# Two cross attentions on one core: two pairs of PSUM banks in turn for scores, values and transposes, later values, and the other work four products ahead

## The chip, the core and the metric

The kernel runs on one core of a Trainium2 chip. The metric is device time in microseconds from the first to the last instruction of one launch, with what the runtime adds around it; lower is better. A core has five engines, each with its own queue that it works through in order: TensorE (in profiles PE, with its weight loads as PEld), VectorE (DVE), ScalarE (ACT), GpSimd (POOL) and SyncE (SP). DMAs are issued from the queues of SP, POOL and ACT. Matmuls write PSUM, 8 banks of 128 partitions x 512 numbers; everything else lies in SBUF or in device memory.

## What is computed

Two cross attentions, one after the other, on x of 4 batches x 1024 rows x 1024 columns (4096 rows in all) against a context of 4 x 64 rows, all in float32:

```
# layer 0: 32 query heads of 32 columns in 8 groups that share keys and values
q, k, v = x @ Wq + bq, ctx @ Wk + bk, ctx @ Wv + bv
p   = softmax(q k^T / sqrt(32) + mask)            # 64 keys
x1  = layernorm((p v) @ Wo + bo + x) * gamma + beta
# layer 1: 16 heads of 64 columns, keys and values from layernorm(ctx)
Q, K, V = x1 @ Wq'^T, a @ Wk'^T, a @ Wv'^T        # a = layernorm(ctx)
p   = softmax(Q K^T / 8, masked)
y   = x1 + tanh(gate) * ((p V) @ Wo'^T)
```

## The kernel before

**Tiling.** The rows are worked on in subtiles of 128 (`SUB` = 8 of them make one of four blocks, `NSUB` = 32 in all). Large products use a scheme with seven block products in place of eight: sums of blocks are made on VectorE, and TensorE multiplies 128 x 512 blocks. A set-up stage makes keys and values and the queries of block 0. Then comes the loop of the first attention, in `mix` (L721). After it the output projection of layer 0 runs over 16 pairs of subtiles (L961), and then scores, softmax and output of layer 1, pair by pair (L1077).

**The loop of the first attention.** `mix(t, steps)` writes down the attention of subtile t and strews other TensorE work between its parts: in blocks 0 to 2 the 28 steps of the next block's query products (`query_steps`, L535; each step is four matmuls of 128 x 512, L541), dealt out 3 or 4 to a subtile, and in block 3 the five steps of `folded_queries` (L822) that turn a chunk of the second layer's query weight on TensorE and multiply it with the keys. `other()` (L728) runs a share of the steps.

Subtile t itself: `front(c)` (L637), for c = 0 and 1, computes half of the scores into a `big` tile (eight matmuls of 64 x 128, L644) and VectorE adds the mask and moves them to SBUF (L648). `largest` finds maxima (L655) and subtracts part of them (L658); `powers` runs the exponentials on ScalarE (L662, L670); `total` sums (L675) and `divide` multiplies with the reciprocal (L679). Then the probabilities have to be turned so that keys lie on partitions. Up to subtile 20 (`by_turning`, L603) they go to device memory (L773, on POOL's queue) and come back as `pq` in quarters (L694, POOL again), and `flip` turns 32 x 32 squares on VectorE (L381). From subtile 21 on `flip` uses transposes on TensorE (L704) and copies on ScalarE (L705). `values(c)` multiplies with the values (L710), copies (L716) and stores the result (L717, SP).

In `mix(t)`, `outputs0(t - 1)` is called after the first score half, so the loads of `pq` stand there; `flip(0)` and `flip(1)` of subtile t-1 stand in the middle, `values(0)` and `values(1)` of t-1 behind the sums and divisions of t.

**PSUM.** Four banks (`wx`) serve the large products. Two single banks (`one`) serve values, transposes and half of the folded values (L860). One pair (`big`) serves both score halves and the other half of the folded values.

**Queries.** The queries of a block are stored to `qTd` by SP and loaded again subtile by subtile (L612), one subtile ahead. The first load of a block stands at the end of the last subtile of the block before (L771); in the first subtile of a block a sixth share of the steps stands ahead of the scores.

**What sets the order.** The order in the text is only a priority. A scheduler orders the instructions of each engine from these priorities, the buffers that are free, and durations of its own; so an engine's order can differ from the text by a subtile or more. It also puts in the waits.

## Time and profile before

| | us |
|---|---|
| runs (3) | 1973.22 median, 1964.64 to 1975.02 |
| the profiled run | 1974.35, of which 1972.6 is the span of its instructions |
| TensorE (PE) busy | 1914.1, 97% |
| VectorE (DVE) busy | 1276.1, 65% |
| ScalarE (ACT) busy | 395.8, 20% |
| GpSimd (POOL) busy | 295.1, 15% |
| mean granted TensorE clock | 0.986 of full |

The loop of the first attention lies from about 195 us (its first scores are at 196.8) to about 755 us (its last values end at 753.4); what follows it takes the rest of the span.

How to read the profile: a row of a timeline gives start and duration in us, the engine, the line of the kernel, the operation, output and input by the names of the tiles, and in brackets how long the engine had been idle before, and who released it. A float32 matmul appears as two rows, so eight score matmuls are sixteen rows. A row of the waits gives waiter and releaser, the sum in us, how often, and the longest. The chain of waits follows the work that ended last back through its releasers. The granted clock is the share of full speed that TensorE was given.

### The profile page before, as it was taken

Reading aid. Unit: us, or ns where it says so; the run is one execution under the profiler, and the core shown is the slowest. Engines: PE = TensorE matmul, PEld = TensorE weight load, DVE = VectorE, ACT = ScalarE, POOL = GpSimd, SP = SyncE. Lnnn points to the kernel's source line nnn. Section 1 sums busy time; section 2 is a strip of 40 time slices with the busy share of each in tenths; the row PEclk is TensorE's granted clock in tenths of the full one; section 3 lists DMA queues with packets and bytes.
Section 4 is the critical chain, followed back from the end, with each engine's and each line's share of the span. In section 5 each row is a group of like instructions: output and inputs, shape, how many; then the busy total and the mean of one; then the engine's idle time right before and its main releaser. Section 6 shows DMA issues by size and latency. Waiting matters only on the chain.

```text
span 1972.6 us, 16687 instructions
## 1 busy us (share of the span) xinstructions
PE 1914.1 (97%) x5872; PEld 888.8 (45%) x5872; DVE 1276.1 (65%) x1540; ACT 395.8 (20%) x1131; POOL 295.1 (15%) x208
## 2 busy tenths in 40 slices
PE   8999999998989899999999999999999999999998
PEld 7744443443434564443443444444444444444443
DVE  3524886887877885445467667657675766576653
ACT  1111652553534673212200000000000000000000
POOL 0000111121110102545555543000000000000000
PEclk9999999998999799999999999999999999999999
DMA  8971699686895688376483335456746574747421
GB/s 279 183 183 63 198 247 239 202 239 210 229 259 186 217 266 291 128 245 213 160 234 139 117 106 128 139 142 157 181 118 161 138 181 117 178 120 181 117 85 43
DMA packets 218917, 346.28 MB, mean 176 GB/s; under 512 B 25425, under 2 KB 140497, under 8 KB 213585
## 3 DMA queue, kind: packets, MB, share of 16 engines
q1 hardware_dynamic: 189824, 271.80, 48.6%
q0 software_dynamic: 9744, 44.05, 8.0%
q10 hardware_dynamic: 19264, 29.37, 5.4%
q8 instruction: 46, 0.75, 0.2%
q14 instruction: 39, 0.31, 0.1%
HBM read 205.44 MB, written 139.72 MB: 175 GB/s over the span
## 4 chain that ended last, share of the span: by engine, by line
PE 67%; DVE 6%; DMA 3%; issue 1%; ACT 1%; POOL 0%; SPq 0%; DVEq 0%; ACTq 0%; POOLq 0%
PE wx L405 58%; PE wx L541 3%; PE one L710 2%; PE one L863 1%; DVE sm L675 1%; PE big L644 1%; DVE s L679 1%; DVE mx L655 1%; PE one L704 1%; DVE s L648 1%; PE big L863 1%; PE wx L836 1%; DMA pq<-p 1%; DMA q<-qTd 1%; DMA xq<-in_x_dram 1%
## 5 line engine op out<-in xcount | busy, mean ns | idle before, releaser
L413 DVE TENSOR_TENSOR r<-wx,r 128x512 f32<-128x512 f32 x224 | 153.6, 686 | 262.0 <-PE wx L405 259.7
L467 ACT ACTIVATE s<-s 128x1024 f32<-128x1024 f32 x32 | 33.7, 1057 | 651.1 <-DVE s L466 642.7
L417 DVE TENSOR_TENSOR s<-wx,key_bias 128x512 f32<-128x512 f32 x64 | 44.1, 690 | 137.3 <-PE wx L405 137.3
L662 ACT ACTIVATE s<-s,mx 128x64 f32<-128x64 f32 x336 | 111.8, 334 | 60.4 <-DVE mx L655 55.8
L541 PE MATMUL wx<-xT,wq_S 128*128 128x512 f32 x256 | 121.7, 608 | 0.8 <-ACT z L552 0.8
L405 PE MATMUL wx<-wo_B,S 128*128 128x512 f32 x256 | 117.0, 599 | 0.4 <-DVE r L413 0.4
L888 POOL TENSOR_TENSOR r<-r,bo 128x1024 f32<-128x1024 f32 x32 | 78.8, 2470 | 256.0 <-DMA r<-in_x_dram 256.0
L541 PE MATMUL wx<-xB,wq_A 128*128 128x512 f32 x256 | 116.9, 599 | 0.0
L405 PE MATMUL wx<-b_B,pT 128*128 128x512 f32 x256 | 116.1, 593 | 0.1
L405 PE MATMUL wx<-b_B,S_p 128*128 128x512 f32 x256 | 115.9, 595 | 0.0
L405 PE MATMUL wx<-a_B,xT 128*128 128x512 f32 x256 | 115.4, 592 | 0.0
L405 PE MATMUL wx<-a_B,S_x 128*128 128x512 f32 x256 | 115.3, 593 | 0.0
L405 PE MATMUL wx<-wo_B,o 128*128 128x512 f32 x256 | 114.1, 596 | 0.0
L648 DVE TENSOR_TENSOR s<-big,m 128x1024 f32<-128x1024 f32 x64 | 77.5, 1211 | 56.3 <-PE big L644 53.5
L644 PE MATMUL big<-kv,q 64*128 64x128 f32 x1024 | 79.0, 291 | 19.9 <-DVE s L648 12.3
L929 POOL TENSOR_TENSOR r<-r,gamma 128x1024 f32<-128x1024 f32 x32 | 76.0, 2376 | 137.2 <-DVE r L285 137.2
L644 PEld LDWEIGHTS big<-kv,q 64*128 64x128 f32 x1024 | 67.2, 194 | 64.1 <-DVE s L648 30.9
L381 DVE STREAM_TRANSPOSE pT<-pq 128x1024 f32<-128x1024 f32 x70 | 82.7, 1217 | 0.0
L710 PE MATMUL one<-pT,kv 128*64 128x512 f32 x256 | 73.0, 667 | 9.0 <-DVE pT L381 8.9
L930 POOL TENSOR_TENSOR r<-r,beta 128x1024 f32<-128x1024 f32 x32 | 80.8, 2523 | 2.4
L679 DVE TENSOR_TENSOR s<-s,sm 128x1024 f32<-128x1024 f32 x64 | 78.7, 1248 | 0.5
L405 PEld LDWEIGHTS wx<-wo_B,S 128*128 128x128 f32 x256 | 47.2, 190 | 66.4 <-issue 54.4
(163 smaller groups left out, 3000.0 us busy)
## 6 DMA issues: line engine op xcount, KB each, us to landing
p<-s POOLq DMA_DIRECT2D x21, 1024.0 KB, 5.9
pq<-p POOLq DMA_DIRECT2D x84, 256.0 KB, 7.1
xq<-in_x_dram SPq DMA_DIRECT2D x64, 256.0 KB, 10.1
q<-qTd SPq DMA_DIRECT2D x32, 512.0 KB, 6.8
oTd<-oT SPq DMA_DIRECT2D x64, 256.0 KB, 4.9
ad<-a SPq DMA_DIRECT2D x16, 1024.0 KB, 6.0
o<-oTd SPq DMA_DIRECT2D x16, 1024.0 KB, 9.0
r<-in_x_dram SPq DMA_DIRECT2D x32, 512.0 KB, 4.1
```

The source lines that it names most:

```text
L381: nc.vector.transpose(dst.rearrange("p k (u i) -> p k u i", i=Q), t[:, :, k0 * Q : k1 * Q].rearrange("p u (k j) -> p k u j", j=Q),)
L405: nc.tensor.matmul(bank, a[s][:, k, :], w[m][:, k, :], start=first and k == 0, stop=last and k == HK - 1, skip_group_check=True,)
L413: nc.vector.tensor_tensor(at, bank, at, ALU.add)
L541: nc.tensor.matmul(bank, w_q[a][:, k, sub_ap(i)], rows[b][:, k, :], start=first and k == 0, stop=last and k == HK - 1, skip_group_check=True,)
L644: nc.tensor.matmul(ps[:, at : at + P], q[on, c * 4 + g, :], k0bd[on, b, c, :], start=True, stop=True,)
L648: nc.vector.tensor_tensor(quarters[:, :, c * 8 : (c + 1) * 8], ps.rearrange("p (k a l) -> p a k l", a=NQ, l=Q), mask.rearrange("p e (h l) ...
L662: nc.scalar.activation(heads[:, 0, k], heads[:, 0, k], AF.Exp, bias=mx[:, 0, k : k + 1], accum_out=sm[:, 0, k : k + 1],)
L679: nc.vector.tensor_tensor(heads[:, e], heads[:, e], wide(sm[:, e]), ALU.mult)
L710: nc.tensor.matmul(ps[i * 64 : (i + 1) * 64, :], v0bd[:, b, c, i, :], pTs[c][:, i * 4 : (i + 1) * 4].rearrange("p g l -> p (g l)"), start= ...
L888: nc.gpsimd.tensor_tensor(ru, ru, bo_sb, ALU.add)
L929: nc.gpsimd.tensor_tensor(r[u], r[u], gamma0_sb, ALU.mult)
L930: nc.gpsimd.tensor_tensor(r[u], r[u], beta0_sb, ALU.add)
```

## The change

The two single banks and the pair become two pairs, and `one()` is now half of a pair. Scores, values and transposes take the pairs in turn; a subtile's values for both halves go into one pair and are copied (1024 columns) and stored at once; `turn` writes eight transposes into one pair and copies once. The other work becomes one generator over all blocks and the folded queries, of which four steps run ahead of the first subtile and eight more between blocks 2 and 3; the first query load of a block stands at the last step of its products. The probabilities' way to memory and back is issued at the end of their own subtile; the turning of t-1 stands behind the first division of t, and the values of turned subtiles come in the subtile after that. `pq` has one buffer in place of two, `outT` two larger ones in place of three.

```diff
-    ps_one = ctx.enter_context(tc.tile_pool(name="ps_one", bufs=2, space=bass.MemoryType.PSUM))
-    ps_big = ctx.enter_context(tc.tile_pool(name="ps_big", bufs=1, space=bass.MemoryType.PSUM))
+    ps_big = ctx.enter_context(tc.tile_pool(name="ps_big", bufs=2, space=bass.MemoryType.PSUM))
...
     def one():
-        return ps_one.tile([P, 512], F32, tag="one", name="one")
+        return big()[:, 0:512]
...
-    def turn(nat, dst, banks=None):
-        for h in range(2):
-            ps = banks[h] if banks else one()
-            for k in range(HK):
-                nc.tensor.transpose(ps[:, sub_ap(k)], nat[:, sub_ap(h * HK + k)], ident)
-            nc.scalar.copy(dst(h), ps.rearrange("p (k l) -> p k l", k=HK))
+    def turn(nat, dst):
+        ps = big()
+        for k in range(KC):
+            nc.tensor.transpose(ps[:, sub_ap(k)], nat[:, sub_ap(k)], ident)
+        nc.scalar.copy(dst, ps.rearrange("p (k l) -> p k l", k=KC))
...
         if by_turning(t):
+            nc.gpsimd.dma_start(out=p0[t], in_=s)
             pq = pqpool.tile([P, NQ, 512], F32, tag="pq", name=f"pq0_{t}")
...
-            for i in range(2):
-                ps = one()
-                for g in range(4):
-                    nc.tensor.transpose(ps[:, sub_ap(g)], s[:, sub_ap((c * 2 + i) * 4 + g)], ident)
-                nc.scalar.copy(pT[:, i * 4 : (i + 1) * 4].rearrange("p g l -> p (g l)"), ps)
+            turn(s[:, c * 1024 : (c + 1) * 1024], pT)
-        def values(c):
-            ps = one()
...
+        def values():
+            oT = opool.tile([P, KC, P], F32, tag="oT", name=f"oT0_{t}")
+            ps = big()
+            for c in range(2):
+                for i in range(2):
+                    nc.tensor.matmul(
+                        ps[i * 64 : (i + 1) * 64, c * 512 : (c + 1) * 512], v0bd[:, b, c, i, :],
...
             nc.scalar.copy(oT.rearrange("p g l -> p (g l)"), ps)
-            nc.sync.dma_start(out=oTd[t // 2][:, c * 4 : (c + 1) * 4, sub_ap(t % 2)], in_=oT)
+            nc.sync.dma_start(out=oTd[t // 2][:, :, sub_ap(t % 2)], in_=oT)
...
-    def mix(t, steps):
+    def mix(t, count):
         front, largest, exps, total, divide = attend0(t)
-        first = t % SUB == 0
-        places = 6 if first else 5
+        places = 5
...
-        if first:
-            other()
         front(0)
-        if t:
-            flip, values = outputs0(t - 1)
         if (t + 1) % SUB:
             load_queries(t + 1)
         other()
         front(1)
...
-        if t:
-            flip(0)
-            flip(1)
+        if t and not by_turning(t - 1):
+            values(t - 2)
+            flip(t - 1)
         powers(1)
         other()
         powers(2)
+        values(t - 2)
         total(1)
         divide(1)
-        if t:
-            values(0)
+        if t and not by_turning(t - 1):
+            values(t - 1)
         other()
+        if t and by_turning(t - 1):
+            flip(t - 1)
         powers(len(exps))
         total(0)
         divide(0)
-        if t:
-            values(1)
+        turned[t] = outputs0(t)
         other()
-        if (t + 1) % SUB == 0 and t + 1 < NSUB:
-            load_queries(t + 1)
-        if by_turning(t):
-            nc.gpsimd.dma_start(out=p0[t], in_=probs[t])
...
-    pqpool = open_pool(attention, "probsq", 2, "right")
+    pqpool = open_pool(attention, "probsq", 1, "right")
     ppool = open_pool(attention, "probsT", 2, "right")
-    opool = open_pool(attention, "outT", 3, "right")
+    opool = open_pool(attention, "outT", 2, "right")
...
-                banks = two() if n else [one(), one()]
+                banks = two()
...
+    def other_work(rows):
+        for blk in range(1, NBLK):
+            steps = query_steps(blk, rows)
...
+            for n, step in enumerate(steps):
+                step()
+                if n in fills:
+                    fills[n]()
+                if n == len(steps) - 1:
+                    load_queries(blk * SUB)
+                yield
...
+        for k in range(KC):
+            ahead = chunk(wq1, k + 1, "wq1") if k + 1 < KC else None
+            for step in folded_queries(kT, wch, k):
+                step()
+                yield
...
+    AHEAD = 4
+    n = 28 * (NBLK - 1) - AHEAD
+    go_on(AHEAD)
+    last = NSUB - SUB
+    for t in range(last):
+        mix(t, (t + 1) * n // last - t * n // last)
+    go_on(2 * AHEAD)
+    n = 5 * KC - 2 * AHEAD
+    for i in range(SUB):
+        mix(last + i, (i + 1) * n // SUB - i * n // SUB)
```

Here `values(u)` and `flip(u)` in `mix` run the kept closures of subtile u if there are any; `go_on(n)` runs n steps of the other work.

More of the change, by code (lines that the diff above doesn't have):

```diff
@@ L700, in flip @@
                 return
-            for i in range(2):
-                ps = one()
-                for g in range(4):
-                    nc.tensor.transpose(ps[:, sub_ap(g)], s[:, sub_ap((c * 2 + i) * 4 + g)], ident)
-                nc.scalar.copy(pT[:, i * 4 : (i + 1) * 4].rearrange("p g l -> p (g l)"), ps)
-        def values(c):
-            ps = one()
-            for i in range(2):
-                nc.tensor.matmul(
-                    ps[i * 64 : (i + 1) * 64, :], v0bd[:, b, c, i, :],
-                    pTs[c][:, i * 4 : (i + 1) * 4].rearrange("p g l -> p (g l)"),
-                    start=True, stop=True,
-                )
-            oT = opool.tile([P, 4, P], F32, tag="oT", name=f"oT0_{t}_{c}")
+            turn(s[:, c * 1024 : (c + 1) * 1024], pT)
[6 more added lines that the diff above has]
+                        ps[i * 64 : (i + 1) * 64, c * 512 : (c + 1) * 512], v0bd[:, b, c, i, :],
+                        pTs[c][:, i * 4 : (i + 1) * 4].rearrange("p g l -> p (g l)"),
+                        start=True, stop=True,
+                    )
             nc.scalar.copy(oT.rearrange("p g l -> p (g l)"), ps)
-            nc.sync.dma_start(out=oTd[t // 2][:, c * 4 : (c + 1) * 4, sub_ap(t % 2)], in_=oT)
+            nc.sync.dma_start(out=oTd[t // 2][:, :, sub_ap(t % 2)], in_=oT)
         return flip, values
-    def mix(t, steps):
+    turned = {}
+    def mix(t, count):
         front, largest, exps, total, divide = attend0(t)
-        first = t % SUB == 0
-        steps = list(steps)
-        places = 6 if first else 5
+        places = 5
         def other():
-            nonlocal places
-            for _ in range(-(-len(steps) // places)):
-                steps.pop(0)()
+            nonlocal count, places
+            for _ in range(-(-count // places)):
+                next(work)
+                count -= 1
             places -= 1
@@ L737, in powers, with values, flip @@
                     exps.pop(0)()
-        if first:
-            other()
+        def values(u):
+            if u in turned:
+                turned.pop(u)[1]()
+        def flip(u):
+            for c in range(2):
+                turned[u][0](c)
         front(0)
-        if t:
-            flip, values = outputs0(t - 1)
         if (t + 1) % SUB:
@@ L789, in tile_two_cross_attentions @@
     spool = open_pool(attention, "scores", 2, "right")
-    pqpool = open_pool(attention, "probsq", 2, "right")
+    pqpool = open_pool(attention, "probsq", 1, "right")
     ppool = open_pool(attention, "probsT", 2, "right")
-    opool = open_pool(attention, "outT", 3, "right")
+    opool = open_pool(attention, "outT", 2, "right")
     load_queries(0)
-    for blk in range(NBLK - 1):
-        steps = query_steps(blk + 1, rows)
-        if blk + 2 < NBLK:
-            rows, fills = rows0(blk + 2)
-            def both(n, fills=fills, steps=steps):
-                steps[n]()
-                if n in fills:
-                    fills[n]()
-            steps = [lambda n=n: both(n) for n in range(28)]
-        for i in range(SUB):
-            lo, hi = i * 7 // 2, (i + 1) * 7 // 2
-            mix(blk * SUB + i, steps[lo:hi] if i < SUB - 1 else steps[lo:])
-    queries_cm.close()
-    fold_cm = ExitStack()
-    fold = open_pool(fold_cm, "fold", 1)
-    early_cm = ExitStack()
-    early = open_pool(early_cm, "early", 1)
     def chunk(w, k, name):
@@ L827, in first @@
         def first():
-            turn(wch, lambda h: wT[:, h * HK : (h + 1) * HK, :])
+            turn(wch, wT)
         def heads(cc):
@@ L890, in load_outputs @@
         return o, r
-    kT = fold.tile([P, KC, B * S], F32, tag="kvT", name="kT")
-    nc.sync.dma_start(out=kT, in_=kTd)
-    wch = chunk(wq1, 0, "wq1")
-    w_o, w_o_sums = right_weight(wo0, "wa", "wo0")
-    bo_sb = constant(bo0.partition_broadcast(P), [P, H], "bo", F32, fold)
-    for i in range(SUB):
-        ahead = chunk(wq1, i + 1, "wq1") if i + 1 < KC else None
-        mix((NBLK - 1) * SUB + i, folded_queries(kT, wch, i))
-        wch = ahead
-        if i == 3:
-            run(w_o_sums)
-        if i == 5:
-            first_outputs = load_outputs(0)
@@ L905, in tile_two_cross_attentions @@
-    flip, values = outputs0(NSUB - 1)
-    for part in (flip, values):
-        for c in range(2):
-            part(c)
+    def other_work(rows):
+        nonlocal fold, early, bo_sb, w_o, first_outputs
+        for blk in range(1, NBLK):
+            steps = query_steps(blk, rows)
+            fills = {}
+            if blk + 1 < NBLK:
+                rows, fills = rows0(blk + 1)
+            for n, step in enumerate(steps):
[5 more added lines that the diff above has]
+                yield
+        queries_cm.close()
+        fold = open_pool(fold_cm, "fold", 1)
+        early = open_pool(early_cm, "early", 1)
+        kT = fold.tile([P, KC, B * S], F32, tag="kvT", name="kT")
+        nc.sync.dma_start(out=kT, in_=kTd)
+        wch = chunk(wq1, 0, "wq1")
+        w_o, w_o_sums = right_weight(wo0, "wa", "wo0")
+        bo_sb = constant(bo0.partition_broadcast(P), [P, H], "bo", F32, fold)
+        for k in range(KC):
[3 more added lines that the diff above has]
+                yield
+            wch = ahead
+            if k == 3:
+                run(w_o_sums)
+            if k == 5:
+                first_outputs = load_outputs(0)
@@ new lines, in tile_two_cross_attentions, with go_on @@
+    fold_cm, early_cm = ExitStack(), ExitStack()
+    fold = early = bo_sb = w_o = first_outputs = None
+    work = other_work(rows)
+    AHEAD = 4
+    def go_on(n):
+        for _ in range(n):
+            next(work)
+    n = 28 * (NBLK - 1) - AHEAD
[5 more added lines that the diff above has]
+    n = 5 * KC - 2 * AHEAD
+    for i in range(SUB):
+        mix(last + i, (i + 1) * n // SUB - i * n // SUB)
@@ L909, in tile_two_cross_attentions @@
+    next(work, None)
+    flip, values = turned.pop(NSUB - 1)
+    for c in range(2):
+        flip(c)
+    values()
     attention.close()
@@ L1045, in turn_at_once @@
         for u in range(2):
-            turn(
-                at_once[pair][:, u], lambda h: pT[:, h * HK : (h + 1) * HK, sub_ap(u)],
-                two() if u else None,
-            )
+            turn(at_once[pair][:, u], pT[:, :, sub_ap(u)])
         return left_out(pT, lppool, f"p_{pair}")
```

## The prediction

> **What bounds the kernel now.** I began with the page: busy shares, then the forty slices.

> ```profile
> PE 1914.1 (97%) x5872; PEld 888.8 (45%) x5872; DVE 1276.1 (65%) x1540; ACT 395.8 (20%) x1131; POOL 295.1 (15%) x208
> ...
> PEclk9999999998999799999999999999999999999999
> ```

> TensorE is busy for 97% of the span, so nothing that only shortens another engine's work can count for much. But one slice of the clock row reads 7, and both it and the gaps of the PE row lie in one place: the first attention, from about 195 to 755 us. I cut that stretch into windows of 25 us (columns: span, busy of PE, PEld, DVE, ACT, POOL, then granted clock, DMA share and GB/s):

> ```profile
> 325.00:350.00 25.00, 22.05 (x75) 9.96 (x73) 6.30 (x7) 2.55 (x5) 2.74 (x5) 0.86 0.63 179
> ...
> 450.00:475.00 25.00, 19.64 (x53) 8.39 (x52) 22.33 (x20) 8.79 (x37) 2.74 (x5) 0.80 0.69 221
> ...
> 575.00:600.00 25.00, 19.99 (x73) 8.45 (x73) 21.46 (x23) 4.44 (x6) 0.00 (x0) 0.93 0.75 192
> ...
> 625.00:650.00 25.00, 18.26 (x137) 12.52 (x134) 17.13 (x17) 11.86 (x22) 0.00 (x0) 0.89 0.93 280
> 650.00:675.00 25.00, 23.02 (x106) 13.32 (x106) 19.79 (x16) 13.17 (x22) 4.99 (x2) 0.64 0.51 171
> ```

> From 200 to 750 us, 22 such windows, PE is busy 512.0 of 550 us: 38.0 us idle. The granted clock falls short of 1 by 1.02 windows in sum, 25.5 us more. These 63.5 us are all that the change can win; after 755 us PE misses hardly anything. The same windows have VectorE busy 445 us of 550: with PE's waits gone it is 90% full, and becomes the second bound.

> The timeline of PE shows how a wait is paid twice:

> ```profile
> 448.33 1.98 PE L541 MATMUL wx<-xB,wq_S 128*128 128x512 f32 x4
> 455.68 1.23 PE L644 MATMUL big<-kv,q 64*128 64x128 f32 x8 [5.37 <-DVE s L648]
> 456.84 1.97 PE L710 MATMUL one<-pT,kv 128*64 128x512 f32 x4
> ```

> The scores wait 5.37 us for the single `big` tile, and afterwards four L710 rows take 1.97 us where they take 1.08 at full clock. The gaps at 338, 450, 578 and 628 us (2.5 to 5.4 us) each do this.

> The waits of VectorE in 195 to 760 us say who holds whom:

> ```profile
> DVE s L648 <- PE big L644: 49.4, 21, 12.7
> DVE sm L675 <- ACT s L670: 23.5, 16, 3.0
> ...
> DVE xT L381 <- DMA xq<-in_x_dram: 5.4, 1, 5.4
> DVE wo_B L175 <- DMA wo_B<-in_wo_dram: 5.0, 1, 5.0
> ...
> DVE s L648 <- DMA p<-s: 2.7, 1, 2.7
> ```

> VectorE waits 49.4 us for scores that PE could not write, because VectorE had not yet emptied the one `big` pair: the two engines take turns. The chain of waits shows the turn in the last subtiles:

> ```profile
> 721.49 1.15 DVE s L648
> 722.63 0.04 issue
> 722.68 1.16 PE big L644 x16
> ```

> An addition empties the pair, only then come 1.16 us of scores, and then the next addition.

> **The change part by part, against the span's own time** (1972.6 us in a run of 1974.35; the median of the runs is 1973.22, 0.06% away). I price it on VectorE's ledger, 106 us of waits in the loop, since PE's are its mirror.

> *Two pairs of banks.* Both score groups of a subtile can now be written before VectorE empties either. In the changed program's order the two groups (2 x 1.09 us) stand side by side from subtile 8 on, with the values of the subtile three earlier just ahead of them. So of the 49.4 us most goes, but a new chain enters: VectorE's turning (L381) -> values (1.87 us for eight rows) -> first score group (1.09) -> VectorE's addition. It is bare where the turning is the last VectorE work before the additions: subtiles 10, 16 and 17, each 1.9+1.1+0.2 = 3.2 us; at 8, 15, 18 and 19 a division (1.25 us) or more lies beside it, leaving 1.8, 1.8, 1.3 and 1.9; at the others over 3 us of VectorE work do. Sum 16.4 us. The second score group needs the pair that the values' copy has just left (about 1.05 us by L670's row for 1024 columns, against 1.09 of the first group): 0.3 us of PE per subtile, not on VectorE's path.

> *The change from turned to PE-transposed probabilities (subtiles 22 to 24).* There the scores of subtile 23 hold both pairs, and the transposes of 22 stand behind them: they wait until VectorE has done two of `w_o`'s sums, an addition and the first score addition (2.27+0.65+2.27+1.2 = 6.4 us). PE then has transposes 2.0, values 1.9, two turns of `wq1` 2.0 and the first folded product 4.0 us to do before the scores of 24, and VectorE needs them 18 us after the division: 6.4+9.9+1.1 = 17.4 at full clock, some 23 with half of it slow. I take 6 us of VectorE wait (0 to 12).

> So 49.4 becomes 16.4+6: **27 us off.**

> *Four products ahead.* The queries of the next block are now loaded before the last products of a subtile, about one subtile (16 us) before use, against q<-qTd's 6.8 us behind qTd's write of 4 to 5: the 12.7 us wait at 338 (counted above) goes. That load holds SP's queue until qTd has landed; behind it stand the next q, mask and qTd writes, none due within a subtile. The eight x loads (L237) come in one run on SP's queue, ahead of the oTd write that held the last one back: 5.4 us off. The wait for p<-s, 2.7 (of 0 to 2.7), I let go as well: p now stands directly ahead of its own pq on POOL. The wait for wo_B stays: its load still follows e's last addition on SP, and 8 us of load stand against about 5 of VectorE work: 4 of the 5.0 remain. **9 us off.**

> *Values two subtiles later, one `pq` buffer.* POOL issues p, then pq when the previous turning has freed the buffer. From that to the next turning is a subtile, 16 to 17 us; issue takes about 2 and the load 7.1 (median) to 14.35 (the longest in the chain of waits). Hidden by 8 us at the median, late by nothing to 1 us at worst; I take 0.

> *Copies.* 64 oT copies of 586 ns become 32 of about 1.05 us, 44 (L705) of 590 become 22, 24 (L376) become 12: 75.6 us of ScalarE become about 69, where it is at most 81% busy (725 to 750 us). I take 0: its waiters wait for the last copy either way. DMAs on SP: 32 fewer.

> *What is late next.* In the changed order 17 more Matmults of the query products (15 us of PE) come before subtile 21 than before it, and fill waits there. A product is eight L541 rows, 3.55 us in the timeline, and a subtile has 3.33 of them now. From subtile 16 to 21 PE then has 5 x (11.8 products + 2.2 scores + 1.9 values) = 80 us of work; VectorE has 5 x (12.2 work + 1.5 wait for exponents) + 9.5 of the chain above + 4 for wo_B = 82 (12.2: 232 us busy from 197 to 488, less 38 for turning x and its sums, over 16 subtiles). Two engines equally full that hand work to each other don't both run without gaps: I take 8 us (0 to 20). After 24 VectorE alone bounds: 12.5 us a subtile against 13.2 now, already in the 27.

> Sum: 27 + 9 - 8 = 28 us; 1974.35 - 28 = **1946 us**. On PE's ledger that is under half of its 63.5 us.

> [...] The trace has the clock at 0.51 over 647.7 to 661 us and 0.52 over 668 to 678.5, stretches with many transposes (L704), though PE was hardly idle within them; after 455 and 583 us, among products, it recovered in 8 and 4 us. [...] But at 680 to 750 us the same transposes run at 1.00.

> **The rivals.**

> 1. *Most of the gain is spent again in the new chain.* If turning, values and scores cost 3.2 us at each of the 13 subtiles 8 to 20, or the pq load comes late there, the chain takes 42 us in place of 16.4, and of 28 us of gain 3 are left: 1971 us. For it: 83.3 us in which POOL waits to issue pq behind p. Against: in six of the thirteen over 3 us of VectorE work lie in between.

> 2. *Slower: the halved clock holds through the last eight subtiles.* Mechanism: transposes wait for a bank pair that holds the next subtile's scores, PE pauses 1 to 2 us in every subtile, and the clock stays at 0.5. In the trace before, the two subtiles that ran like this took 21.3 and 18.7 us (second score groups at 643.0, 664.3, 683.0) against 13.2: 20.0 in the mean, 7.5 over the 12.5 forecast. From four such subtiles the gain is used up; from six it is slower by over 0.5%; with eight, 8 x 7.5 = 60 less 28: 2006 us. Against: from 696 us on PE paused 0.9 to 1.4 us in every subtile at full clock.

> 3. *Both engines nearly close up.* No slow stretch, no coupling loss: the floors are 57.5 products x 3.55 + 32 score groups x 1.09 + 14 values x 1.88 = 265 us (subtiles 0 to 15), 80 (16 to 20), and for VectorE 11 x 12.3 + 14 of turning, sums and additions + 8 of last transposes and values = 157; 502 against 556.6 now (196.8 to 753.4): 54 us, 1920 us. For it: two pairs give PE a whole subtile of lead.

> **How the numbers follow.** Forecast (1932 to 1958) 0.56; rival 3 (below 1932) 0.17; rival 1 (1958 to 1975) 0.18; rival 2, with any other loss, 0.09. The range takes in the floors and rival 1 and leaves out rival 2: 1918 to 1972. This kernel's time can be told from no change from about 0.5% on, 10 us. Of rival 1 a third (0.06) gains over 10 us, and of the last 0.09 one in nine loses under 10. So faster 0.79, within 0.5% 0.13, slower 0.08.

> **What would show it.** Right: "DVE s <- PE big" falls below 30 us; no PE gap over 3 us at the block changes; the clock row shows no 7; fronts of subtiles 28 to 31 follow each other in about 12.5 us; 0 to 195 us and everything after the loop unchanged. Wrong: PE waiting for L381 before the values in most subtiles (rival 1); windows after the first folded product at a clock of 0.5 to 0.6 (rival 2); VectorE's turning waiting for pq<-p (the one buffer).

## The result, and the profile after

Six runs of the changed kernel took 1955.88 to 1958.85 us, median 1956.68, against 1974.12 (1964.64 to 1975.8) for six runs of the kernel before. The ratio is 0.9924, 95% interval 0.9902 to 0.9946: faster by 17.4 us between the medians and by 14.9 between the means, which the ratio follows. The forecast was 28 us, so the direction held and the size did not. The profiled run took 1957.66 us with a span of 1955.9. The runs of the kernel before scatter with the clock: in 49 later ones (1960.9 to 1976.9 us) the mean granted clock goes from 0.994 in the shortest to between 0.985 and 0.987 in the longest, and the profiled run, 1974.35 us at 0.986, is among the long ones, where the changed kernel's six have 0.990 or 0.991.

The same rows of the page of the changed kernel as were shown of before:

```profile
PE 1885.4 (96%) x5872; PEld 886.9 (45%) x5872; DVE 1271.4 (65%) x1540; ACT 386.9 (20%) x1065; POOL 294.5 (15%) x208
...
PEclk9999999998999999999999999999999999999999
```

Read the first row as a ledger of TensorE. The span fell by 16.7 us, yet PE did not wait less: its idle time (span less busy) rose from 58.5 to 70.5. What fell is its *busy* time, by 28.7 us, with the same 5872 instructions; how much of this a shorter run of the kernel before would show is not known, since no trace of one was kept. By groups, the folded products went from 49.8 to 36.8 us, the values from 73.0 to 66.8, the transposes of the probabilities from 28.6 to 22.9. Many of those rows ran at half clock before, between 647 and 679 us; that stretch is gone, and the 7 of the clock row with it. The gain lies almost wholly in the last eight subtiles: from the first scores of subtile 24 to the last values of the loop it took 123.2 us (630.2 to 753.4) and now takes 110.4 (626.5 to 736.9); everything ahead of subtile 24 gained only 3.7. Of the 16.7 us of span 16.5 are there when the loop ends (753.4 and 736.9). (The first scores of the kernel before are at 190.8 us, not at 196.8; those of the changed kernel, behind four products, at 194.6.)

The waits of VectorE from 195 to 740 us in the changed kernel (waiter, releaser, sum, times, longest):

```profile
DVE s L646 <- PE big L642: 56.3, 20, 12.1
DVE sm L673 <- ACT s L668: 16.7, 15, 1.6
DVE e L556 <- PE wx L539: 6.2, 1, 6.2
DVE wo_B L174 <- DMA wo_B<-in_wo_dram: 4.2, 1, 4.2
```

The wait for scores, which the two pairs were to end, did not fall: 56.3 us against 49.4. The waits for x and for p are gone, and that for `wo_B` is 4.2, as forecast. Why the first row grew is told by PE's own waits, first of the kernel before from 195 to 760 us, then of the changed kernel in the same stretch as above:

```profile
PE big L644 <- DMA q<-qTd: 7.2, 3, 2.9
```

```profile
PE big L642 <- DMA q<-qTd: 13.2, 2, 7.5
PE big L373 <- DVE s L646: 7.9, 5, 2.3
PE big L708 <- DVE pT L379: 6.2, 5, 4.2
```

Two waits for the first queries of a block now cost 13.2 us, where the kernel before had 7.2 in three, and both VectorE's stalls of over 10 us (10.66 and 12.07) stand behind them. The clock makes both dearer. Windows of 25 us of the changed kernel (span, busy of PE, PEld, DVE, ACT, POOL, granted clock, DMA share, GB/s):

```profile
325.00:350.00 25.00, 19.32 (x84) 10.12 (x82) 12.98 (x13) 5.38 (x15) 3.68 (x7) 0.86 0.80 216
...
475.00:500.00 25.00, 17.46 (x92) 10.08 (x92) 14.67 (x15) 7.96 (x35) 2.73 (x5) 0.80 0.64 183
```

These two windows alone lose 5.7 + 7.5 us of PE's time to idleness and (0.14 + 0.20) x 25 = 8.5 us to the clock.

### The profile page after: what moved, and what is told of

The parts are those of the page before. It is cut to its first block, busy times and chain, and to the rows that moved or that the text cites. A ratio compares the mean times of both kernels' runs of the same rounds, so it can differ in the third digit from the quotient of the medians.

```text
span 1955.9 us, 16585 instructions
## 1 busy us (share of the span) xinstructions
PE 1885.4 (96%) x5872; PEld 886.9 (45%) x5872; DVE 1271.4 (65%) x1540; ACT 386.9 (20%) x1065; POOL 294.5 (15%) x208
## 4 chain that ended last, share of the span: by engine, by line
PE 66%; DVE 6%; ACT 2%; issue 2%; DMA 1%; SPq 0%; ACTq 0%; DVEq 0%
PE wx L403 59%; PE wx L539 3%; PE big L842 1%; DVE mx L653 1%; DVE s L646 1%; PE big L642 1%; DVE s L656 1%; DVE sm L673 1%; PE big L708 1%; PE big L373 1%; DMA q<-qTd 1%; DVE s L677 0%; ACT b L847 0%; PE wx L815 0%; ACT oT L713 0%
## 5 line engine op out<-in xcount | busy, mean ns | idle before, releaser
L646 DVE TENSOR_TENSOR s<-big,m 128x1024 f32<-128x1024 f32 x64 | 77.2, 1218 | 56.3 <-PE big L642 56.3
L642 PE MATMUL big<-kv,q 64*128 64x128 f32 x1024 | 81.8, 297 | 21.0 <-DMA q<-qTd 13.2
L694 POOL DMA_DIRECT2D pq<-p x84 | 45.8, 552 | 205.2 <-DVE pT L379 145.3
## 6 DMA issues: line engine op xcount, KB each, us to landing
xq<-in_x_dram SPq DMA_DIRECT2D x64, 256.0 KB, 10.2
q<-qTd SPq DMA_DIRECT2D x32, 512.0 KB, 8.4
oTd<-oT SPq DMA_DIRECT2D x32, 512.0 KB, 7.1
r<-in_x_dram SPq DMA_DIRECT2D x32, 512.0 KB, 4.2
```

Of the source, the lines that this page charges most:

```text
L642: nc.tensor.matmul(ps[:, at : at + P], q[on, c * 4 + g, :], k0bd[on, b, c, :], start=True, stop=True,)
L646: nc.vector.tensor_tensor(quarters[:, :, c * 8 : (c + 1) * 8], ps.rearrange("p (k a l) -> p a k l", a=NQ, l=Q), mask.rearrange("p e (h l) ...
L694: nc.gpsimd.dma_start(out=pq[a * Q : (a + 1) * Q], in_=v[a])
```

## The experiments

The change has three parts that can be had apart: the two pairs of banks, the products that run ahead, and the values that come a subtile later. The rest of the new order (one generator, the query load at the last product, one `pq` buffer) goes with all kernels of the table but the first two and has no run of its own. The first seven runs make a table of them; the rest take away the wait for the queries. The runs of the kernel before scatter by 11 to 14 us in each set of runs (medians of 1966.7 to 1974.1), so the ratios to it, each taken within one set on one chip, are compared, and not the microseconds. The last three columns are waits in us, from 195 to 750 or 760 us, in the profiled run: PE for a query load, PE for turned probabilities before the values, VectorE for scores.

| kernel | banks | products ahead | values later | ratio, 95% interval | q | turned | scores |
|---|---|---|---|---|---|---|---|
| before | old | no | no | 1 | 7.2 | 8.9 | 49.4 |
| b_banks | pairs | no | no | 1.0113, 1.0090 to 1.0137 | 0 | 37.0 | 65.7 |
| a_vals1 | pairs | 4 | no | 1.0126, 1.0104 to 1.0149 | 0 | 49.5 | 62.6 |
| a_ahead0 | pairs | no | yes | 0.9979, 0.9965 to 0.9994 | 0.2 | 28.6 | 36.4 |
| the change | pairs | 4 | yes | 0.9924, 0.9902 to 0.9946 | 13.2 | 6.2 | 56.3 |
| o_vals1 | old | 4 | no | 1.0035, 1.0020 to 1.0049 | 21.8 | 9.5 | 58.1 |
| o_ahead0 | old | no | yes | 0.9927, 0.9907 to 0.9947 | 0 | 7.6 | 35.9 |
| a_oldbanks | old | 4 | yes | 0.9942, 0.9922 to 0.9961 | 2.5 | 13.8 | 32.3 |

(0: not among the waits that the view lists. The profiled run of o_vals1, 1981.49 us, is the longest of its twelve, whose median is 1974.62.)

**b_banks: the two pairs alone.** The kernel before with

```diff
-    ps_one = ctx.enter_context(tc.tile_pool(name="ps_one", bufs=2, space=bass.MemoryType.PSUM))
-    ps_big = ctx.enter_context(tc.tile_pool(name="ps_big", bufs=1, space=bass.MemoryType.PSUM))
+    ps_big = ctx.enter_context(tc.tile_pool(name="ps_big", bufs=2, space=bass.MemoryType.PSUM))
...
-            values(0)
+            values()
...
-        if t:
-            values(1)
```

with the new `turn`; `values()` computes both halves into one pair, which is copied and stored by halves; so the second half's values also stand one place earlier.

> The kernel before with the two pairs of banks alone (and what they bring: eight transposes to a pair, values of a subtile in one pair behind the first division); no products ahead, values still of the subtile before, two pq buffers. Theory, from the two traces: TensorE's busy time fell by 28.7 us (1914.1 to 1885.4) and its idle time rose by 12.0 (58.5 to 70.5); 25 of the 28.7 lie in rows of the last subtiles that ran at half clock before (folded products 49.8 to 36.8, transposes 28.6 to 22.9, values 73.0 to 66.8). If two pairs end that half-clock stretch by themselves, this gives most of the gain: 1958 to 1966 us, folded products near 37, and VectorE's wait for scores below 40. Rival: the order (values later, other work ahead) ended it: 1970 to 1978 us, folded products still near 50.

Measured: 1.1% slower. Folded products fell to 41.1, towards the 37 of the first theory, and it was still wrong: the half clock lay elsewhere, mostly between 590 and 624 us (0.66 and 0.59 granted in the windows of 25 us from 575 to 625). PE's timeline there:

```profile
583.49 1.96 PE L642 MATMUL big<-kv,q 64*128 64x128 f32 x28
600.33 1.97 PE L705 MATMUL big<-pT,kv 128*64 128x512 f32 x4 [14.87 <-DVE pT L379]
602.23 0.80 PE L642 MATMUL big<-kv,q 64*128 64x128 f32 x4
...
618.68 1.97 PE L705 MATMUL big<-pT,kv 128*64 128x512 f32 x4 [11.04 <-DVE pT L379]
```

Scores, values and nothing else: the query products have run out. PE's order of instructions says it too. Ahead of the scores of subtile 16 stand 90 products in the kernel before and in the changed one, 98 here; all 112 are done before subtile 20 here, before subtile 24 and 23 there. Until 570 us no gap of PE was over 2.3 us, so nothing looked wrong; but it had been fed products, attention had fallen behind (second score group of subtile 16 at 507.2 us against 492.4), and the last turned subtiles then ran bare, each one a whole chain of scores, softmax, way through memory, turning and values, with PE waiting 14.87 and 11.04 us for the turning. Why the scheduler puts more products ahead when there are two pairs was not followed, and no run held them back: that the loss comes of it is read from this trace.

**a_vals1: the changed kernel with the values directly behind the turning.**

```diff
-        values(t - 2)
...
             flip(t - 1)
+            values(t - 1)
```

> The changed kernel with the values of turned probabilities directly behind their turning, not a subtile later. Theory of the prediction: turning to values to scores becomes one chain: TensorE's wait for the turned probabilities grows from 6.2 us to 15 to 30 and the time to 1962 to 1975. Rival: values two subtiles later gain nothing, since TensorE has the other products to do in between: wait under 10 us, time 1952 to 1960.

Measured: 1.3% slower than before, 2% behind the changed kernel; the loss was larger than either theory had. It is the same failure as in b_banks, one subtile earlier (102 products ahead of subtile 16, all 112 done before subtile 19):

```profile
PE big L708 <- DVE pT L379: 49.5, 8, 16.4
```

**a_oldbanks: the changed order on the banks of before.**

```diff
-    ps_big = ctx.enter_context(tc.tile_pool(name="ps_big", bufs=2, space=bass.MemoryType.PSUM))
+    ps_one = ctx.enter_context(tc.tile_pool(name="ps_one", bufs=2, space=bass.MemoryType.PSUM))
+    ps_big = ctx.enter_context(tc.tile_pool(name="ps_big", bufs=1, space=bass.MemoryType.PSUM))
```

with `turn`, `values` and copies by halves as before.

> The changed order (four products ahead, values two subtiles later, one pq buffer) on the banks of before (two single ones and one pair), copies by halves as before. Theory (banks end the half-clock stretch): no gain or a loss, 1970 to 1990 us, a stretch at half clock around subtiles 22 to 25 and folded products near 50. Rival (the order did it): 1953 to 1962, folded products near 37.

Measured: 0.9942. The rival held: the order makes the gain without the pairs. The first theory, that the pairs ended the half-clock stretch and so brought the gain, fell here: the stretch is gone with the old banks too (every window of 25 us from 575 to 750 us has 1.00).

**o_ahead0: the values later, nothing ahead** (a_oldbanks with `AHEAD = 0`). The rest of the new text stays: one generator, the query load at the last product, one `pq` buffer.

> Banks of before, values a subtile later, no product ahead. The run with old banks and the whole new order gained 0.58% and the one with new banks and values at once lost 1.26%, so the theory that the two pairs bring the gain has fallen. Theory now: the later values alone carry it: ratio to before 0.992 to 0.998 here, TensorE's wait for the turned probabilities under 20 us. Rival: the four products ahead carry it, on old banks at least: ratio 0.998 to 1.005.

Measured: 0.9927, the whole gain of the change, by the later values and the rest of the new order together. Up to 550 us it has no gap of PE of 1.5 us and no window under full clock, where the kernel before paused for 2.95, 2.78, 5.37 and 1.70 us and had windows at 0.86, 0.80 and 0.93. The second score group of subtile 16 comes at 473.9 us in place of 492.4, with 90 products ahead of it in both. Behind 550 us stand gaps of 6.86 (at 551.72) and 4.23 us; the first comes up again below. The largest of its PE waits from 195 to 560 us:

```profile
PE big L644 <- DVE s L648: 7.9, 3, 6.9
PE one L712 <- DVE pT L381: 3.1, 7, 0.9
```

**o_vals1: only the products ahead** (a_oldbanks with the edit of a_vals1).

> Banks of before, four products ahead, values of turned probabilities directly behind their turning. Theory (values later are worth some 33 us only where pairs are shared, because there the values take one of two pairs from the scores): with values in banks of their own the loss is small: ratio 0.994 to 1.002. Rival (values later are worth this much whatever the banks): ratio 1.008 to 1.015 and query products used up by subtile 20, as with the two pairs.

Measured: 1.0035. With banks of their own, values directly behind the turning cost less than with the pairs, but more than the theory's bound; and what I had called the cure of the block change made that wait largest of all, 21.8 us in four waits.

Two comparisons of the table differ in the place of the values alone: o_vals1 with a_oldbanks (0.9%) and a_vals1 with the change (2.0%). Each is more than the whole gain of the change. What goes with them is not the same: with the old banks the wait for queries (21.8 to 2.5 us), with the pairs the wait for turned probabilities (49.5 to 6.2). The pairs lose 1.1%, 0.9% and 0.5% (b_banks, a_vals1 and a_ahead0 beside their neighbours with the old banks), and lie within the intervals, 0.2% ahead, only where both other parts are there (0.9945 in the second set of runs of the change, below, takes that lead away).

**a_ahead0: the changed kernel with nothing ahead** (the eight steps between blocks 2 and 3 go as well, since they are `2 * AHEAD`).

> The changed kernel with no product ahead (AHEAD = 0). The wait for the first queries of a block did not go (13.2 us on TensorE against 7.4 before). Theory: it hangs on SP's queue and on the late last addition, and a distance of four products hardly matters: wait for q<-qTd 10 to 18 us, time 1952 to 1963. Rival: the four products are what keeps it from growing: wait over 22 us, time over 1968.

Measured: 0.9979; the products ahead are worth 0.55% with the pairs (0.34% beside the second set, 0.9945, whose interval just meets this one). Neither theory had it right: the wait for the queries went from 13.2 to 0.2 us, and the wait for turned probabilities came up to 28.6 in its place. With the pairs, the products ahead shorten the end of the loop: from the first scores of subtile 24 to the last values it takes 123.2 us before, 121.4 in b_banks and 118.7 here, but 110.4 in the changed kernel and 112.5 in a_vals1, which have products ahead. An estimated 5 to 7 us of the difference to b_banks and to a_ahead0 is work moved: in the two with products ahead 31 of the 256 rows of the folded products (36.8 us in all) and 16 turns of `wq1` (8.7 us for 64) stand ahead of subtile 24, in the other two no such row and 8 or 0 turns. With the old banks the products ahead bring nothing there: 124.3 (a_oldbanks) and 125.7 (o_vals1) with them, 122.5 (o_ahead0) without. Nor do they decide where the clock is halved: the windows of 25 us between 600 and 650 us run at 0.80 and 0.80 here, at 0.84 and 0.86 in o_ahead0 and at 1.00 in a_oldbanks, but at 0.64 and 0.76 in a_vals1.

**a_oTact and a_z3: the wait for the queries.** Two things stand ahead of a block's first query load. SP's queue in the changed kernel, about subtile 8 and about subtile 16:

```profile
322.51 0.33 SPq L553 DMA_DIRECT2D qTd<-e  x1
325.87 0.53 SPq L714 DMA_DIRECT2D oTd<-oT  x1
326.50 4.85 SPq L610 DMA_DIRECT2D q<-qTd  x2
...
468.35 0.32 SPq L553 DMA_DIRECT2D qTd<-z  x1
470.01 0.52 SPq L714 DMA_DIRECT2D oTd<-oT  x1
472.44 5.11 SPq L610 DMA_DIRECT2D q<-qTd  x2
```

At subtile 8 the load goes out behind a store of values that waits for its copy, ten microseconds after the last queries were stored (316.15). At subtile 16 it goes out four microseconds after the last queries, which were late themselves. VectorE, about subtile 16:

```profile
462.05 2.28 DVE L177 TENSOR_TENSOR xN<-xB,xT 128x2048 f32<-128x2048 f32 x1
464.25 1.22 DVE L656 TENSOR_TENSOR s<-s,mx 128x1024 f32<-128x1024 f32 x1
465.38 2.37 DVE L379 STREAM_TRANSPOSE pT<-pq 128x1024 f32<-128x1024 f32 x2
467.67 0.65 DVE L556 TENSOR_TENSOR z<-wx,z 128x512 f32<-128x512 f32 x1
```

The last addition (`z`) stands behind the sums for the block after next (L175 to L177) and a turning. So one run moves the stores (a_oTact):

```diff
-            nc.sync.dma_start(out=oTd[t // 2][:, :, sub_ap(t % 2)], in_=oT)
+            nc.scalar.dma_start(out=oTd[t // 2][:, :, sub_ap(t % 2)], in_=oT)
```

and one the addition and the load (a_z3):

```diff
-            order += [(p, i) for p in (p6, p7, p5, p3, p4)]
+            order += [(p, i) for p in (p6, p7, p5, p4, p3)]
-        return r, {17: first_half, 25: b12, 26: b22}
+        return r, {17: first_half, 26: b12, 27: b22}
...
+                if n == len(steps) - 1:
+                    load_queries(blk * SUB)
                 if n in fills:
                     fills[n]()
-                if n == len(steps) - 1:
-                    load_queries(blk * SUB)
```

> The changed kernel with the stores of the values' results (L714) on ScalarE's queue. Theory for subtile 8: its first query load stood on SP behind a store of subtile 5's values (issued 325.87, load at 326.50) though the queries had landed at about 321: the 5.7 us gap of TensorE there falls under 1.5, the 7.5 us gap at subtile 16 stays, and with it 5 to 9 us come off: 1948 to 1953 us. Rival: the load waits for the last stored queries themselves; both gaps stay, 1955 to 1959.

> The changed kernel with the last two products of each part swapped, so that the last VectorE addition before a block's query load (z) stands ahead of the next block's sums and turnings and not behind them, and the load ahead of these in the text. Theory for subtile 16: the last addition was late on VectorE (467.7), its store landed at 472.4 and the load went out at 472.44: the 7.5 us gap falls under 2, the one at subtile 8 stays or shrinks little, 6 to 12 us come off: 1945 to 1951. Rival: the sums come late instead and TensorE waits for them by as much: 1954 to 1962.

Measured: a_oTact 0.9915 (0.9896 to 0.9935), 1952.1 us; the gap at subtile 8 went from 5.68 to 3.48, not under 1.5 (the load now stands behind `e` at 322.32 alone), the one at 16 from 7.47 to 6.94. a_z3 0.9871 (0.9849 to 0.9893), 1942.8 us: both gaps are gone. SP and PE of a_z3 about subtile 16:

```profile
451.01 0.32 SPq L553 DMA_DIRECT2D qTd<-z  x1
452.15 0.38 SPq L613 DMA_DIRECT2D m<-in_mask_dram  x1
458.64 1.29 SPq L610 DMA_DIRECT2D q<-qTd  x2
```

```profile
462.07 2.11 PE L708 MATMUL big<-pT,kv 128*64 128x512 f32 x8 [0.85 <-DVE pT L379]
464.11 2.39 PE L642 MATMUL big<-kv,q 64*128 64x128 f32 x32
466.43 1.98 PE L539 MATMUL wx<-xT,wq_S 128*128 128x512 f32 x4
```

The addition went from 467.67 to 450.31, the load from 472.44 to 458.64, and the scores of subtile 16 run at 464.11 with no wait, where they stood at 482.56. The wait for scores on VectorE is 35.3 us in place of 56.3, and the second score group of subtile 24 comes at 614.3 us, near o_ahead0 (616.5), where the changed kernel had it at 631.7 and the kernel before at 634.8: in the changed kernel most of what could be won up to there had been eaten, and the wait for the queries stands in that stretch. At subtile 8 I had expected the gap to stay; with its load ahead of the stores on SP (311.79) it went as well.

**Four more on one chip: after_again, o_z3, o_late_z3, a_z3_oT.** after_again is the changed kernel once more; o_z3 is a_oldbanks with the edit of a_z3; o_late_z3 the same with `AHEAD = 0`; a_z3_oT has both edits of the last paragraph.

> The changed kernel once more, on the same chip as the three that follow, so that they are compared with it and not across chips. Both theories: ratio to before 0.990 to 0.995, the gaps for q<-qTd at subtiles 8 and 16 again 5 to 8 us.

> The whole new order with the swapped last products, on the banks of before. Theory: the two pairs are worth nothing once the order is changed, in either sign: within 0.3% of the kernel with the two pairs and the swap, 0.985 to 0.990 of before. Rival: the two pairs do pay as soon as the block change no longer covers it: 0.991 to 0.996 here, as on old banks without the swap (0.9942), whose wait for q<-qTd was only 2.5 us.

> The smallest set: banks of before, nothing ahead, values a subtile later, and the swapped last products. Theory: the queries then come in time although no product runs ahead, and it is as fast as the best: 0.985 to 0.990. Rival: without products ahead the first load of a block is bare again: 0.991 to 0.996, PE waiting 4 us or more for q<-qTd or for scores at a block change.

> The changed kernel with the swap and with the values' results stored from ScalarE's queue. The swap alone removed both waits for q<-qTd, so if the stores only cost by that wait, nothing is left to gain: 0.986 to 0.988 of before. Rival: SP's queue is late elsewhere too (wo_B, masks): 0.982 to 0.985.

| kernel | median, us | ratio, 95% interval | q | turned | scores |
|---|---|---|---|---|---|
| after_again | 1958.49 | 0.9945, 0.9924 to 0.9967 | 13.0 | 7.8 | 55.7 |
| o_z3 | 1962.49 | 0.9962, 0.9947 to 0.9976 | 7.1 | 10.2 | 33.6 |
| o_late_z3 | 1946.70 | 0.9875, 0.9853 to 0.9896 | 6.6 | 4.7 | 27.9 |
| a_z3_oT | 1944.36 | 0.9869, 0.9845 to 0.9892 | 0 | 1.5 | 33.3 |

On one chip the edits that end the wait for the queries are worth 1958.49 - 1944.36 = 14.1 us. a_z3_oT is no faster than a_z3 (0.9869 and 0.9871), as if the stores cost only by that wait, though it also waits 9.1 us for `wo_B`, where a_z3 waits 2.9. o_z3 went against my theory. The pairs are worth 0.9% over the old banks there, and the swap gained nothing on the old banks with four products ahead (0.9942 without it, intervals that overlap); its largest rows are a wait for `wo_B` of 11.1 us on VectorE, after which PE stood 8.25 us for the turning, and a gap of 4.53 for the queries at subtile 16. o_late_z3 reached the best kernels' time with the old banks, though with 4.18 us of wait at subtile 8.

That run also shows that the swap does more than end a wait for queries. Beside o_ahead0, which has no such wait, it took the ratio from 0.9927 to 0.9875, while a wait for queries of 6.6 us came up. What is gone in o_late_z3 is VectorE's wait for `wo_B`, beside which o_ahead0 has PE's longest gap:

```profile
551.42 2.29 DVE L175 TENSOR_TENSOR wo_B<-wo_B,wo_B 128x2048 f32<-128x2048 f32 x1 [7.21 <-DMA wo_B<-in_wo_dram]
558.58 2.08 PE L644 MATMUL big<-kv,q 64*128 64x128 f32 x16 [6.86 <-DVE s L648]
```

In a_oldbanks, whose time the swap did not better, the two are 10.51 and 11.40 us. So the 14.1 us is a price of the edits, not shown to be that of the wait for queries alone, and part of the differences between kernels with the old banks may be this load; no run moved it by itself.

So two ways lead to the same 0.987: pairs, four products ahead, values later and the swap, or old banks, nothing ahead, values later and the swap. Both beat the two kernels of this case: 1.25 and 1.3% under the kernel before, and 11.8 and 14.1 us under the changed kernel on the same chip. What does not settle is a price for the pairs or for the products ahead that holds by itself: the sign of the one turns with the other, and every edit makes the scheduler write another order.

## Why the prediction was right in direction and wrong in size

**"Two pairs of banks ... 27 us off" failed, and with it the reason I gave for the gain.** I read "DVE s <- PE big 49.4" as a shortage of banks. The pairs alone made that wait 65.7 us and the kernel 1.1% slower. The wait names PE's score matmuls, but in b_banks what held them was PE's queue: an engine that works in order writes scores when its order comes to them, and 98 products stood ahead of subtile 16 in place of 90. The old banks with the later values have 32.3 and 35.9, the lowest of the first table; the pairs with later values and nothing ahead have 36.4.

**"Values two subtiles later, one `pq` buffer ... I take 0" is the term that carried the gain.** I priced its DMA (rightly: no turning waited for `pq` in the changed kernel) and counted the later values only as a part of the new chain, turning to values to scores, 16.4 us of loss. The runs show the opposite: with the pairs, values at once make PE wait 49.5 us for the turning, a subtile later 6.2; with the old banks they cost 0.9%. That the pairs need the later values, or lose, was in none of my cases. Why the same move ends another wait on the old banks than on the pairs stays open; no run followed the scheduler's choice. Both comparisons have four products ahead; without these the later values were tried only together with the rest of the new order (o_ahead0, 0.9927).

**The wait for the queries at 338, "the 12.7 us wait ... goes", failed.** I reckoned from the place of the load in the text to its use, "about one subtile", and said that nothing due soon stands behind it. What counted stood *ahead*: SP's queue, and VectorE's last addition behind three sums and a turning. It is the term that was mis-sized: in place of 0 it cost 13.2 us of gaps and 8.5 of clock, and the edits that removed it brought 14.1, with whatever else they moved. That is about the size of the miss (10.6 us by the medians, 13.1 by the means); with it gone the time is 1942.8, beside the 1946 forecast. This is agreement of a sum, not of its terms, and so partly luck.

**What held.** x and p waits gone, `wo_B` 4.2 (4 forecast). The copies: ScalarE 395.8 to 386.9, though the scores now wait in two places for a pair that a copy of values has to leave, 4.7 us of PE in all, where I had put 0.3 a subtile. The stretch behind the loop: 1219.2 us before, 1219.0 now. Subtiles 28 to 31 follow each other in 12.2, 11.1 and 14.2 us, 12.5 in the mean, as forecast. From the first scores of 16 to those of 21 it took 86.4 us, between the 82 of work and the 90 with 8 of coupling.

**The marks I had set.** "Falls below 30 us" and "no PE gap over 3 us at the block changes" both failed (56.3; 5.68 and 7.47 us), and they pointed at the right two steps; the clock row without a 7 and the late subtiles held. Rival 2 did not come: the stretch with 32 transposes at subtile 24, 606 to 668 us, ran at full clock. Whether such transposes hold a clock at half once it is there was not put to the test, since the clock was already full when they began. The sign of rival 1, PE waiting for the turning, is what a_vals1 and b_banks show, but no rival of mine held their mechanism: filler that is used up too early.

## What to carry to other kernels

A wait that names an engine in order says when its turn came, and need not mean that a buffer was short; before pricing more buffers, count in the order of the queue what stands ahead of the waiting instruction, and how long the filler lasts. A value that is needed only much later can be made later by one stage of the loop, so that its producer's chain lies beside other work; here, with four products ahead, that move was worth 0.9 to 2.0%, and the whole change 0.76%. And follow a load backwards to the instruction that makes its data: the place of the load in the text says nothing while the last addition stands behind work that has time.

## What the runs showed of the hardware

The four sets of runs of the kernel before have medians from 1966.7 to 1974.1 us, but within each set the runs lie 11 to 14 us apart, so it is not shown that the chips differ. The changed kernel came to 0.9924 of it in one set and to 0.9945 (11.9 us between the medians) in another: a difference of a few tenths of a per cent is readable only between kernels that ran beside each other, and with their intervals.
